# A selective-scan kernel on Trainium2: summing over the states by accumulating fp32 transposes

## The chip, the cores and the metric

The kernel runs on one core of a Trainium2 chip. The metric is the device time of one execution in microseconds (us). A core has five engines that run side by side and wait for each other by semaphores: TensorE (PE; its weight loads are listed apart as PEld), VectorE (DVE), ScalarE (ACT), GpSimd (POOL) and SyncE (SP), which here only issues transfers. TensorE writes to PSUM, an accumulator memory of eight banks of 128 partitions x 512 fp32 values; a matmul holds one operand still in the array (it is loaded first) and streams the other through it.

## The reference, cut to what matters

Eight images of 96 channels and 64 x 64 pixels pass through a Mamba-like layer, an attention without softmax and a quantised feed-forward network. Nearly all the time goes to the selective scan of the first layer: 192 inner channels, 4096 positions, four directions and 16 states for each channel.

```python
def step(h, t):
    u_t, d_t, B_t, C_t = t
    dA = jnp.exp(d_t[..., None] * A)
    h = dA * h + (d_t * u_t)[..., None] * B_t[:, :, None, :]
    y = jnp.einsum('bkdn,bkn->bkd', h, C_t)
    return (h, y)
```

Here n runs over the 16 states. The change concerns the last sum: y is the sum over n of h times C.

## The kernel before, in words

The images go in four pairs. For each pair, `front` does the norms, the input projection and the depthwise convolution, `scan` the selective scan in four directions, `back` the output norm, gate and projection, and `tail` the attention and feed-forward network. The 192 channels of two images fill three tiles of 128 partitions.

`scan` cuts the 4096 positions into 8 chunks of 512. A step is one chunk in one direction, so there are 32 steps for a pair; each step has three tiles T and each tile 16 states n. The innermost piece of work, a unit, is one (step, tile, state): 48 units make a step, 6144 the kernel. A unit has three parts:

- `unit_a`: two bf16 matmuls spread row n of B and of C over the 128 partitions, into the PSUM tiles pb (L322) and pcc (L324). ScalarE computes da, the exponential of delta times A (L326), VectorE multiplies pb by du in place (L329), and ScalarE copies pcc to cc in SBUF (L331).
- `unit_b`: VectorE runs the recurrence over the 512 positions as one scan instruction (L342), GpSimd multiplies the result by cc, which gives hc (L344), and after every fourth state ScalarE saves the last column (L347).
- `unit_c`: TensorE adds hc to the PSUM tile py by a matmul with the identity (L352). After the 16th state VectorE adds py to y (L357 in the first direction, L362 in the others).

The loop at the end of `scan` hands out part a of unit i, part b of unit i - 1 and part c of unit i - 3. Between the units it slips in what the next tile or step needs: `project` makes B and C and the low-rank step input of a new step with two sets of three fp32 matmuls (L268), ScalarE's copies (L272, L277), VectorE's split into bfloat16 parts (L274, L278) and one GpSimd subtraction (L279). `step_size` makes delta and du for one tile with a small fp32 matmul ptd (L285), five ScalarE functions (L290 to L297), one VectorE instruction (L299) and three GpSimd products (L300, L301, L303).

A scheduler of the framework orders each engine's instructions, and every engine then runs its list in that order. In the list of TensorE, pb stands four units ahead of py: after py of unit i comes pb of unit i + 4, often with a pcc beside it. Buffers limit how far the engines drift apart: pb has three PSUM banks, pcc and py two each, and the eighth bank, tag "m", is shared by the projections and ptd; da, cc and hc have three SBUF buffers each.

Of the kernel before, what the change touches and what calls it, by code (L numbers as in the profile page):

```python
# [21 lines left out]
NS = 16  # L22
# [10 lines left out]

# Two images share three 128-partition tiles of the 192 inner channels:
#   tile 0: image 0, channels 0..127      tile 1: image 1, channels 0..127
#   tile 2: channels 128..191 of image 0 (partitions 0..63) and of image 1 (64..127)


@with_exitstack
def vss_attn_ffn(ctx: ExitStack, tc: tile.TileContext, a: dict):  # L40
# [11 lines left out]

    # one table set for all but Silu
    nc.scalar.preload_act_table_set(LOGEXP)
# [29 lines left out]

    # A = -exp(A_log); the sum over the directions of D, as all four read the same u
    amat = load("alog", [128, KD, 2, NS])
# [4 lines left out]

    # FFN weights and biases in the 5-bit exponent, 2-bit mantissa format
    w1q = const.tile([DIM, HID], F8, name="w1q")
# [23 lines left out]

# [1 line left out]
    def front(pair, xi, zs, ybuf):  # L119
        with ExitStack() as st:  # L120
# [52 lines left out]

            # Silu from here on, in a table set of its own
            for b in range(2):
# [51 lines left out]

# [1 line left out]
    def scan(xi, y):  # L229
        with ExitStack() as st:  # L230
# [8 lines left out]
            def view(t, k, c):  # L239
                """Chunk c of an image in the order of direction k (before its flip)."""  # L240
                if k % 2 == 0:
                    return t[:, bass.ts(c, F)].rearrange("p (h w) -> p h w", w=HH)
                return t.rearrange("p (h w) -> p w h", w=HH)[:, bass.ts(c, ROWS), :]
# [16 lines left out]
            def project(s, g):  # L260
                """B (g = 0, with the step's low rank) or C: rows 0..31, 64..95 and 96..127 of S
                get the high, middle and low bfloat16 parts, whose sum is the float32 value."""
                k, c, _ = steps[s]
                if g == 0:
                    S[s] = pr.tile([128, 2, F], BF16, name="S", bufs=2)
                pt = psm.tile([128, F], F32, name="pt", tag="m")
                for T in range(3):
                    nc.tensor.matmul(  # L268
                        pt, xw[k][:, g, T, :], view(xi[T], k, c), start=(T == 0), stop=(T == 2)
                    )  # L270
                Sg = S[s][:, g]
                nc.scalar.activation(Sg, pt, AF.Copy)  # L272
                R = pr.tile([128, F], F32, name="R")
                nc.vector.tensor_tensor(R[64:128], pt[64:128], Sg[64:128], ALU.subtract)  # L274
                if g == 0:
                    dts[s] = pr.tile([128, F], F32, name="dts")
                    nc.scalar.activation(dts[s][32:44], pt[32:44], AF.Copy)  # L277
                nc.vector.tensor_copy(Sg[64:128], R[64:128])  # L278
                nc.gpsimd.tensor_tensor(Sg[96:128], R[96:128], Sg[96:128], ALU.subtract)  # L279

            def step_size(s, T):
                """delta = softplus(dts + bias) = max(v, 0) + log1p(exp(-|v|)), and delta * u."""
                k, c, _ = steps[s]
                pt = psm.tile([128, F], F32, name="ptd", tag="m")
                nc.tensor.matmul(  # L285
                    pt, dtw[k][32:44, T, :], dts[s][32:44], start=True, stop=True
                )
                bias = dtb[:, k, half(T) : half(T) + 1]
                r = pr.tile([128, F], F32, name="r")
                nc.scalar.activation(r, pt, AF.Relu, bias=bias)  # L290
                e = pr.tile([128, F], F32, name="e")
                nc.scalar.activation(e, pt, AF.Abs, bias=bias)  # L292
                nc.scalar.activation(e, e, AF.Exp, scale=-1.0)
                u = pr.tile([128, F], F32, name="u")
                nc.scalar.activation(u, e, AF.Identity, bias=1.0)
                d = pr.tile([128, F], F32, name="delta", bufs=2)
                nc.scalar.activation(d, u, AF.Ln)  # L297
                # what 1 + e lost in rounding
                nc.vector.scalar_tensor_tensor(u, u, -1.0, e, ALU.add, ALU.subtract)  # L299
                nc.gpsimd.tensor_tensor(d, d, u, ALU.subtract)  # L300
                nc.gpsimd.tensor_tensor(d, d, r, ALU.add)  # L301
                q = pr.tile([128, F], F32, name="du", bufs=2)
                nc.gpsimd.tensor_tensor(rows(q), rows(d), view(xi[T], k, c), ALU.mult)  # L303
                delta[s, T], du[s, T] = d, q

            def feed(s, T):
                """What must have run before tile T of step s, in parts."""
                if s >= len(steps):
                    return []
                k, _, first = steps[s]  # L310
                parts = []
                if T == 0:
                    if first:
                        weights(k)
                    parts += [lambda: project(s, 0), lambda: project(s, 1)]
                return parts + [lambda: step_size(s, T)]

            def unit_a(s, T, n):
                """dA = exp(delta A), dB u = delta u B in PSUM, and C spread over the partitions."""
                k = steps[s][0]  # L320
# [28 lines left out]

            def unit_c(s, T, n, py, hc):  # L350
                k, c, _ = steps[s]
                nc.tensor.matmul(py, ident, hc, start=(n == 0), stop=(n == NS - 1))  # L352
                if n < NS - 1:
                    return
                yv = view(y[T], k, c)
                if k == 0:
                    nc.vector.scalar_tensor_tensor(  # L357
                        yv, view(xi[T], k, c), dsum[:, half(T) : half(T) + 1], rows(py),
                        ALU.mult, ALU.add,
                    )  # L360
                else:
                    nc.vector.tensor_tensor(yv, yv, rows(py), ALU.add)  # L362

# [27 lines left out]

# [1 line left out]
    def back(pair, y, zs, t1):  # L393
        with ExitStack() as st:
# [5 lines left out]
            def mix(m, srcs, T, ps):  # L400
                """The matrices of m take the tiles that hold tile T's images to tile T."""
                use = {0: ((0, 0), (1, 2)), 1: ((0, 1), (2, 2)), 2: ((3, 0), (4, 1), (5, 2))}[T]
                for i, (w, t) in enumerate(use):
                    nc.tensor.matmul(
                        ps, m[:, w, :], srcs[t], start=(i == 0), stop=(i == len(use) - 1)
                    )
# [40 lines left out]

# [1 line left out]
    def tail(pair, t1):  # L449
        with ExitStack() as st:  # L450
# [19 lines left out]

            # a row of ones under the tokens carries the biases
            tn = [big.tile([DIM + 1, L], F32, name=f"tn{b}") for b in range(2)]
            for b in range(2):
                nc.gpsimd.memset(tn[b][DIM : DIM + 1], 1.0)

            # (q k') v = q (k' v): transposed, (k' v)' = v' k for all heads at once
            pm = [psm.tile([128, F], F32, name=f"pm{b}", tag=f"pm{b}") for b in range(2)]
            nblk = L // 128
            for c in range(NCH):
                for b in range(2):  # L480
                    norm(t1[b][:, bass.ts(c, F)], tn[b][0:DIM, bass.ts(c, F)])
                for b in range(2):
                    for i in range(2 * c, 2 * c + 2):
# [10 lines left out]
                        for j in range(2):  # L494
# [3 lines left out]
                            )  # L498
            # the heads' blocks, times the scale; then Wq (k' v) Wff as one matrix
            hm = []  # L500
# [45 lines left out]

            # three chunks at a time, each one part behind the one before it
            going = []
# [6 lines left out]
    for pair in range(npair):  # L555
        zs = dram.tile([3, 128, L], F32, name="zs")
        with tc.tile_pool(name="yp", bufs=1) as yp:
            # the zero-padded input of the convolution, and then the scan's sums
            ybuf = [yp.tile([128, (HH + 2) ** 2], F32, name=f"y{T}") for T in range(3)]
            y = [t[:, :L] for t in ybuf]  # L560
            with tc.tile_pool(name="xip", bufs=1) as xp:
                xi = [xp.tile([128, L], F32, name=f"xi{T}") for T in range(3)]
                front(pair, xi, zs, ybuf)
                scan(xi, y)
            with tc.tile_pool(name="t1p", bufs=1) as tp:
                t1 = [tp.tile([DIM, L], F32, name=f"t1_{b}") for b in range(2)]
                back(pair, y, zs, t1)
                tail(pair, t1)
# [3 lines left out]
def _lay_out(i):  # L572
# [4 lines left out]
    def two(v):  # L577
        """[192, ...] -> [128, 2, ...]: channels 0..127, and 128..191 twice."""
        v = np.asarray(v, f)
# [56 lines left out]

    # constants of the shapes
    e = np.arange(DIM)
# [44 lines left out]
```

## Time and profile before

| | before |
|---|---|
| median of 2 runs | 16719.02 us (16713.03 to 16725.01) |
| span of the profiled execution | 16699.4 us |
| busy: PE, DVE, ACT, POOL | 84%, 76%, 59%, 59% |
| mean granted TensorE clock | 0.906 |
| the four scans together | 13317 us |

The profiled execution's span, from its first to its last instruction, is 16699.4 us, some 20 us below the median of the runs; the difference is what lies around the program. The granted clock is the share of TensorE's full clock that its throttle lets through; in the records it is 1.0 or 0.5 at any one time. An fp32 matmul appears in the trace as two records, each with a weight load of its own, and py of one unit is such a pair. Busy time of TensorE is modelled from the starts of the matmuls and reads too high; distances from start to start tell more.

### The profile page before, as it was taken

The numbers are of one execution on the slowest core, as the hardware profiler recorded it, in microseconds if no ns is written. First come the engines' busy times: TensorE is split into PE (matmuls) and PEld (weight loads), VectorE is DVE, ScalarE is ACT, GpSimd is POOL, SyncE is SP. The second block draws the span as 40 slices with busy tenths as digits, with TensorE's granted clock in tenths as the row PEclk, the third lists the DMA queues.
The fourth block names the chain that finished last, engine by engine and source line by source line (L and its number), as shares of the span: only waits on it lengthen the run. The fifth ranks groups of instructions, "written<-read, shape, count | busy, mean of one in ns | idle before, by whom it ended". The sixth has DMA issues, their size and how long they took to land. (4 is left out here: it accounts for less than half of the span.)

```text
span 16699.4 us, 126308 instructions
## 1 busy us (share of the span) xinstructions
PE 14068.0 (84%) x32636; PEld 4820.2 (29%) x32640; DVE 12648.8 (76%) x14809; ACT 9813.3 (59%) x17754; POOL 9871.6 (59%) x7738
## 2 busy tenths in 40 slices
PE   8888888888988888888898888888889888888888
PEld 2222222223222222222332222222233222222223
DVE  0898899883189889988318988998830898899883
ACT  2666666663266666666326666666632666666663
POOL 0677777772067777777106777777710677777771
PEclk9999999997799999999779999999977999999997
DMA  1000000000000000000000000000000000000001
GB/s 31 2 2 1 2 1 1 1 1 29 24 2 2 1 1 1 1 1 0 30 24 2 2 0 2 1 1 1 1 30 26 0 2 0 2 1 1 1 1 31
DMA packets 48735, 106.06 MB, mean 6 GB/s; under 512 B 7075, under 2 KB 7940, under 8 KB 47108
## 3 DMA queue, kind: packets, MB, share of 16 engines
q1 hardware_dynamic: 48004, 97.97, 2.0%
q8 instruction: 256, 4.19, 0.1%
q14 instruction: 475, 3.89, 0.1%
HBM read 60.21 MB, written 37.75 MB: 6 GB/s over the span
## 5 line engine op out<-in xcount | busy, mean ns | idle before, releaser
L344 POOL TENSOR_TENSOR hc<-h,cc 128x512 f32<-128x512 f32 x6144 | 7831.6, 1280 | 3405.2 <-DVE h L342 2561.7
L352 PE MATMUL py<-hc,ident 128*128 128x512 f32 x12288 | 7244.3, 673 | 1992.9 <-POOL hc L344 1968.2
L342 DVE TENSOR_TENSOR_SCAN h<-da,st,pb 128x512 f32<-128x512 f32 x5376 | 6839.4, 1272 | 11.3
L331 ACT ACTIVATE cc<-pcc 128x512 f32<-128x512 f32 x6144 | 3665.9, 597 | 3446.6 <-POOL hc L344 2798.5
L329 DVE TENSOR_TENSOR pb<-pb,du 128x512 f32<-128x512 f32 x6144 | 4184.9, 681 | 1296.2 <-PE pb L322 1268.9
L326 ACT ACTIVATE da<-delta,c_alog 128x512 f32<-128x512 f32 x6144 | 4414.6, 719 | 497.2 <-DVE h L342 461.7
L352 PEld LDWEIGHTS py<-hc,ident 128*128 128x128 f32 x12288 | 2131.0, 202 | 4978.2 <-POOL hc L344 4475.7
L322 PE MATMUL pb<-S,c_sel 128*128 128x512 bf16 x6140 | 2449.9, 399 | 145.1 <-DVE h L342 141.8
L324 PE MATMUL pcc<-S,c_sel 128*128 128x512 bf16 x6144 | 2348.9, 398 | 5.2 <-POOL S L279 2.5
L279 POOL TENSOR_TENSOR S<-R,S 32x512 bf16<-32x512 f32 x256 | 295.7, 1155 | 1838.5 <-DVE S L278 948.1
L324 PEld LDWEIGHTS <-c_sel 128*128 128x128 bf16 x6144 | 628.6, 102 | 2303.6 <-issue 2250.3
L274 DVE TENSOR_TENSOR R<-pt,S 64x512 f32<-64x512 f32 x256 | 177.8, 695 | 1307.3 <-ACT S L272 1300.0
L322 PEld LDWEIGHTS <-c_sel 128*128 128x128 bf16 x6144 | 631.4, 103 | 1777.1 <-issue 1772.9
L268 PE MATMUL pt<-xi,xw 128*128 128x512 f32 x1536 | 1125.5, 825 | 21.1 <-DMA xw<-in_xw_dram 9.9
L342 DVE TENSOR_TENSOR_SCAN h<-da,pb 128x512 f32<-128x512 f32 x768 | 924.6, 1209 | 5.9
L217 PE MATMUL pc<-y,diag 128*128 128x512 f32 x1728 | 748.1, 595 | 0.0
L544 POOL TENSOR_TENSOR ot<-t,y 96x512 f32<-96x512 f32 x64 | 73.5, 1149 | 951.7 <-DVE y L542 936.7
L300 POOL TENSOR_TENSOR delta<-delta,u 128x512 f32<-128x512 f32 x384 | 486.7, 1267 | 155.2 <-DVE u L299 155.2
L303 POOL TENSOR_TENSOR du<-delta,xi 128x512 f32<-128x512 f32 x384 | 535.5, 1394 | 21.3
L301 POOL TENSOR_TENSOR delta<-delta,r 128x512 f32<-128x512 f32 x384 | 486.6, 1267 | 30.1
L222 ACT ACTIVATE xi<-pc,c_convb 128x512 f32<-128x512 f32 x96 | 66.0, 687 | 681.9 <-PE pc L217 681.9
L285 PE MATMUL ptd<-dts,dtw 12*128 12x512 f32 x768 | 439.7, 652 | 25.1 <-ACT e L292 21.2
(115 smaller groups left out, 8068.9 us busy)
## 6 DMA issues: line engine op xcount, KB each, us to landing
z<-zs SPq DMA_DIRECT2D x32, 768.0 KB, 4.9
zs<-zt SPq DMA_DIRECT2D x64, 256.0 KB, 2.0
xt<-in_x_dram SPq DMA_DIRECT2D x8, 1536.0 KB, 9.4
xr<-in_x_dram SPq DMA_DIRECT2D x32, 384.0 KB
out_dram<-ot SPq DMA_DIRECT2D x64, 192.0 KB, 2.1
zs<-zt SPq DMA_DIRECT2D x64, 128.0 KB
xw<-in_xw_dram SPq DMA_DIRECT2D x16, 384.0 KB, 3.1
c_sel<-in_sel_dram SPq DMA_DIRECT2D x1, 1536.0 KB
```

Of the source, the lines that this page charges most:

```text
L217: nc.tensor.matmul(pc, diag[:, half(T), t, :], pad[T][:, r0 + dy : r0 + dy + ROWS, dx : dx + HH], start=(t == 0), stop=(t == 8),)
L268: nc.tensor.matmul(pt, xw[k][:, g, T, :], view(xi[T], k, c), start=(T == 0), stop=(T == 2))
L300: nc.gpsimd.tensor_tensor(d, d, u, ALU.subtract)
L303: nc.gpsimd.tensor_tensor(rows(q), rows(d), view(xi[T], k, c), ALU.mult)
L322: nc.tensor.matmul(pb, sel[:, T, n, :], S[s][:, 0], start=True, stop=True)
L324: nc.tensor.matmul(pc, sel[:, T, n, :], S[s][:, 1], start=True, stop=True)
L326: nc.scalar.activation(da, delta[s, T], AF.Exp, scale=amat[:, k, half(T), n : n + 1])
L329: nc.vector.tensor_tensor(pb, pb, du[s, T], ALU.mult)
L331: nc.scalar.activation(cc, pc, AF.Copy)
L342: nc.vector.tensor_tensor_scan(hs[:, d], da[:, d], pb[:, d], init, ALU.mult, ALU.add)
L344: nc.gpsimd.tensor_tensor(hc, hs, cc, ALU.mult)
L352: nc.tensor.matmul(py, ident, hc, start=(n == 0), stop=(n == NS - 1))
```

## The change

The sum over n is no longer made by multiplying hc with the identity. In the changed kernel hc is the operand that is loaded into the array, in four pieces of 128 columns, and the identity is streamed through, in TensorE's transpose mode; so py collects the transposed pieces, summed over the 16 states. After the 16th state ScalarE copies py to an SBUF tile yt, four more transposes turn it back into a PSUM tile p2, which takes its bank from tag "m", and VectorE adds p2 to y where it added py. Only the first of the 64 transposes of a tile clears the bank.

```diff
             def unit_c(s, T, n, py, hc):
                 k, c, _ = steps[s]
-                nc.tensor.matmul(py, ident, hc, start=(n == 0), stop=(n == NS - 1))
+                for j in range(4):
+                    js = bass.ts(j, 128)
+                    nc.tensor.matmul(
+                        py[:, js], hc[:, js], ident, is_transpose=True, skip_group_check=True,
+                        start=(n == 0 and j == 0), stop=(n == NS - 1),
+                    )
                 if n < NS - 1:
                     return
+                yt = pr.tile([128, F], F32, name="yt")
+                nc.scalar.activation(yt, py, AF.Copy)
+                p2 = psm.tile([128, F], F32, name="p2", tag="m")
+                for j in range(4):
+                    js = bass.ts(j, 128)
+                    nc.tensor.transpose(p2[:, js], yt[:, js], ident)
                 yv = view(y[T], k, c)
                 if k == 0:
                     nc.vector.scalar_tensor_tensor(
-                        yv, view(xi[T], k, c), dsum[:, half(T) : half(T) + 1], rows(py),
+                        yv, view(xi[T], k, c), dsum[:, half(T) : half(T) + 1], rows(p2),
                         ALU.mult, ALU.add,
                     )
                 else:
-                    nc.vector.tensor_tensor(yv, yv, rows(py), ALU.add)
+                    nc.vector.tensor_tensor(yv, yv, rows(p2), ALU.add)
```

The scheduler places the instructions of the changed kernel anew. pb still stands four units ahead of py on TensorE; the back transposes of a tile stand between py of the second and third unit of the tile after it (or beside py of its first unit); the three matmuls of a projection fall between other units than before. GpSimd's list is nearly the same, and SyncE's transfers are the same in number.

## The prediction

> **What bounds the kernel now.** I read the page's busy line first, then the costliest groups, then the waits, then a table by stage, then the timeline of one place where VectorE stands still.
>
> ```profile
> PE 14068.0 (84%) x32636; PEld 4820.2 (29%) x32640; DVE 12648.8 (76%) x14809; ACT 9813.3 (59%) x17754; POOL 9871.6 (59%) x7738
> ...
> L352 PE MATMUL py<-hc,ident 128*128 128x512 f32 x12288 | 7244.3, 673 | 1992.9 <-POOL hc L344 1968.2
> L342 DVE TENSOR_TENSOR_SCAN h<-da,st,pb 128x512 f32<-128x512 f32 x5376 | 6839.4, 1272 | 11.3
> ...
> L329 DVE TENSOR_TENSOR pb<-pb,du 128x512 f32<-128x512 f32 x6144 | 4184.9, 681 | 1296.2 <-PE pb L322 1268.9
> ```
>
> TensorE looks the busiest, but its ends are modelled. VectorE is the engine to follow: its scan never waits (11.3 us), and its product pb*du waits 1268.9 us, all for the matmul that spreads B (L322). The table by stage, first the scan of the first pair of images, then four short stretches and one of the next pair's in_proj:
>
> ```profile
> 453.00:3786.00 3333.00, 2797.67 (x6693) 946.58 (x6694) 2999.36 (x3386) 2197.66 (x4020) 2394.53 (x1884) 0.94 0.00 1
> ...
> 955.10:958.50 3.40, 1.15 (x5) 0.33 (x4) 3.40 (x5) 0.93 (x3) 3.32 (x4) 1.00 0.00 0
> 958.50:961.90 3.40, 2.29 (x5) 0.83 (x6) 2.51 (x3) 2.25 (x6) 3.40 (x3) 0.67 0.00 0
> 961.90:965.30 3.40, 3.40 (x7) 1.11 (x6) 1.88 (x2) 1.88 (x4) 1.30 (x2) 0.50 0.00 0
> 965.30:968.70 3.40, 3.40 (x11) 1.45 (x9) 2.72 (x4) 2.30 (x6) 1.93 (x2) 0.83 0.00 0
> ...
> 4300.00:4400.00 100.00, 100.00 (x103) 20.13 (x102) 0.00 (x0) 35.18 (x52) 0.00 (x0) 0.50 0.17 51
> ```
>
> The column after the five engines is the granted clock. The four scans take 13317 us of the 16699: 6144 units (step, tile, state), 128 steps of 48 units, 104.0 us a step. Undisturbed, scans start 1.77 us apart (957.87 after 956.10), VectorE back to back. So 48 x 1.77 = 85 us, some 9 us of VectorE's other work (L299, L362, L274, L278), and 1268.9/128 = 9.9 us of waiting. Where the waiting comes from, in the timeline:
>
> ```profile
> 958.27 1.27 POOL L303 TENSOR_TENSOR du<-delta,xi 128x512 f32<-128x512 f32 x1
> ...
> 958.37 1.13 PE L352 MATMUL py<-hc,ident 128*128 128x512 f32 x2 [1.91 <-POOL hc L344]
> ...
> 959.74 0.70 DVE L329 TENSOR_TENSOR pb<-pb,du 128x512 f32<-128x512 f32 x1 [0.61 <-PE pb L322]
> ...
> 960.81 2.08 PE L352 MATMUL py<-hc,ident 128*128 128x512 f32 x2 [1.11 <-POOL hc L344]
> ...
> 962.68 0.63 PE L322 MATMUL pb<-S,c_sel 128*128 128x512 bf16 x1
> ...
> 963.35 0.70 DVE L329 TENSOR_TENSOR pb<-pb,du 128x512 f32<-128x512 f32 x1 [1.73 <-PE pb L322]
> ```
>
> GpSimd's three products for the next step size (L300, L301, L303, 3.9 us) hold up hc; TensorE, in order, stands at py; its clock falls to 0.50; the next py then takes 960.81 to 962.68, 1.87 us instead of 0.96 (2006.80 to 2007.76), and pb comes late three times: by 0.61, by 1.73 and, at 965.98, by 0.75: 3.1 us. Three such places a step make up nearly all of the 9.9 us.
>
> **What the skill says.** "TensorE: Matmul & The Clock Gate", Terms, says that the transpose mode is 4 times faster for fp32. The trace has no transpose; the present py is two records, each streaming 512 columns in 0.43 us at full clock, so a quarter of its rate would be one pass of 0.053 us for 128 columns. The same page, section LDWEIGHTS, prices a load by its columns, 107 ns for 128; the trace has 0.107 us between the two loads of one py at full clock, but 0.166 at half. Its Part 4 says that transposes don't count as activity that lifts the clock; no run shows that yet. "PSUM — Partial Sum Buffer", Part "The four PSUM rules", says that an fp32 transpose sets the written bits as a matmul does, so the sum over 16 states should accumulate as meant.
>
> **The change part by part.**
>
> Removed: per unit, one py of 0.96 us at full clock (0.107 of exposed load, 2 x 0.427), 1.87 at half.
>
> Added per unit: four loads of a piece of hc, each with a 128-column matmul. At full clock with loads behind matmuls: 4 x 0.107 + 0.053 = 0.48 us. At half: 0.161 exposed, 3 x 0.166, 0.107: 0.77. Not in the trace are the price of a transpose's pass and whether its load hides. L486, with new weights for each pass, runs 8 passes at 0.16 us each, its loads hidden; that is the lower bound. The upper bound is serial: 4 x (0.107 + 0.053) = 0.64 at full, 4 x (0.166 + 0.107) = 1.09 at half. Two passes as now would double the loads: 8 x 0.107 + 0.107 = 0.96 at full, no gain.
>
> The clock decides. I weighed the trace's matmul records in windows of 3.41 us, streaming time at full clock times the share of rows and columns used. In the scans, all 64 windows at full clock with 0.30 to 0.32 had lost it in the next, and all 24 with 0.42 to 0.44 kept it; at half, none below 0.33 got it back and all above 0.39 did. The last stage line above fits: TensorE 100% busy with 96 rows, clock 0.50. Today a unit in steady state has (0.853 + 0.427)/1.77 = 0.72. After, pb and pcc alone have 0.427/1.77 = 0.24; with transposes counted at one pass, (0.427 + 0.213)/1.77 = 0.36, on the border. I take the scan to be at half clock for most of its length; only the fp32 projections (L268, 0.85 us a matmul at full) lift it for a window.
>
> At half clock a unit then costs TensorE 0.85 for pb and pcc, 0.77 for the transposes and 0.05 for the next load: 1.67 with loads hidden; backlogged serial loads make it 1.93. I take 1.80, nearer to the hidden end, as L486 shows hiding. That is above VectorE's 1.77. Per step: 48 x 1.80 = 86.4; six projection matmuls at 1.71: 10.3; three ptd at 1.87: 5.6; three sets of back transposes at 0.8: 2.4; sum 104.7. Windows lifted by the projections give back some 2. TensorE still stands at py in three bunches, where the queue holds only four pb ahead: 3 x 1.5 = 4.5 not filled. Sum 107.2 against 104.0: +3.2 x 128 = +410 us.
>
> The rest. ScalarE copies yt 384 times at 0.60 (L331's price): 230 us, on an engine 59% busy; it stands behind a cc in the queue, where cc waits for hc anyway. The back transposes wait for yt; behind them on TensorE stand py and pb of the next tile. At two of three tile ends they fall into a bunch, where py waits 3 to 4 us: free. At the third, yt follows cc34 and pb35 stands behind p2: from the scan's end 0.2 + 1.3 + 0.6 + 0.6 + 1.0 + 0.7 = 4.4 us against VectorE's 4.9 until it needs pb35: free by 0.5 us, else up to 1 us a step, 128 us. VectorE's add into y reads p2 instead of py, same size, no cost. p2 shares the single buffer "m" with the projections and ptd, so these now wait for VectorE's add; at unit 33 three projections follow each other behind it, 5 us at half clock, with pb37 behind: 0.5 us of waiting now, up to 2 then. Inside the 1.5 per bunch I count it. Queues of SP and GpSimd keep their work; front, back and tail are not touched.
>
> Span 16699 + 410 = 17109; the runs' median lies 20 above the profiled span: 17130.
>
> **Rivals.**
>
> A, half clock but loads all hidden: TensorE fits into 1.77. The bunches then wait 4 + 2 + 1.1 + 1.5 us a step by the same walk through the queues, 1 more for p2: 9.6 against 9.9, about 16.7 ms, no change. For it: L486. Against it: only 0.10 us of slack a unit in an in-order queue.
>
> B, the clock stays full (transposes count, 0.36 just holds, or a backlog lifts it: 1.28/1.50 = 0.85 at half is above 0.78). Each bunch waits about 1.5 us: 5 a step, 99 us, -640 us: 16.05 ms, faster. If VectorE never waited, 94 us and 15.4 ms: the floor. It decides where the activity is above 0.38. Against it: the skill's sentence and the sum of 0.24.
>
> C, serial loads, or a switch of mode that drains the array: 1.93 a unit: 92.6 + 10.3 + 5.6 + 3.3 + 1 = 113 us a step, +1150: 17.9 ms. Two passes stuck at half clock (8 loads of 0.166): about 2.2 a unit, over 19 ms.
>
> D, the transposes run as two passes at full rate: TensorE as today, clock full; only the back transposes come on top: 16.7 to 17.0.
>
> **How the numbers follow.** The forecast's case 0.35, A 0.2, B 0.22, C 0.15, D 0.08. Slower by over 2% (above 17053, about what a measurement of this kernel tells from no change) takes most of the forecast's case, C and a little of A and D: 0.53. Faster: B, 0.22. Within: 0.25. The range from 16000 to 18300 takes in A, B's main value and C's serial end; the floor and the two-pass end are left out.
>
> **What would show it.** Right: the mean clock of the scan falls from 0.94 to 0.5 to 0.65; transposes come as one load and one matmul each (24576 + 1536 records); VectorE's waiting for pb spreads over all units instead of three bunches. Wrong: scans 1.77 us apart outside the bunches at half clock (A); a clock above 0.8 in the scan (B); 49152 records (C or D); intervals between transposes above 0.27 us.

## The result, and the profile after

The changed kernel takes 16877.08 us (16873.15 to 16881.01, two runs) against 16719.02: a ratio of 1.0093, 95% interval 1.0063 to 1.0122. It is slower, but by less than the 2% from which the prediction counted its chances. Its profiled execution spans 16871.2 us against 16699.4, 172 more. (Each listed run takes only some 2 us longer than its span; the 20 us between the span before and the median of its runs come from one execution to the next, then, and not from what lies around the program.) The four scans hold the loss: from the first to the last scan instruction of each pair, 13320 us before and 13489 after, 169 more.

The busy line and the costliest groups of the page after (columns as before: busy us, mean ns | idle us ahead of the group, releaser):

```profile
PE 12396.1 (73%) x46460; PEld 5923.0 (35%) x46464; DVE 12550.7 (74%) x14809; ACT 10035.9 (59%) x18138; POOL 9908.5 (59%) x7738
...
L355 PE MATMUL py<-ident,hc 128*128 128x128 f32 x24576 | 4557.9, 314 | 3826.1 <-POOL hc L344 3811.3
L342 DVE TENSOR_TENSOR_SCAN h<-da,st,pb 128x512 f32<-128x512 f32 x5376 | 6825.7, 1271 | 10.4
...
L329 DVE TENSOR_TENSOR pb<-pb,du 128x512 f32<-128x512 f32 x6144 | 4179.4, 682 | 1544.4 <-PE pb L322 1518.3
```

The sum itself became cheap: TensorE's busy time falls from 14068.0 to 12396.1 us although it has 42% more records, and py is 24576 records, one pass for each transpose. Yet VectorE's product (L329) waits longer for pb: 1518.3 us, not 1268.9. The table by stage, scan of the first pair:

```profile
453.00:3786.00 3333.00, 2350.09 (x10003) 1206.28 (x10003) 2932.71 (x3340) 2226.10 (x4066) 2374.98 (x1861) 0.88 0.00 1
```

The granted clock in the scan is 0.88, before 0.94: lower, but far from one half. VectorE is busy 2932.71 us of the 3333, before 2999.36: less is done in the same stretch. Where it stands is shown by the timeline of one bunch of GpSimd products (start us, length us, engine, line; in brackets the idle time before and what ended it):

```profile
980.41 1.26 POOL L303 TENSOR_TENSOR du<-delta,xi 128x512 f32<-128x512 f32 x1
...
982.95 0.66 PE L355 MATMUL py<-ident,hc 128*128 128x128 f32 x4 [3.62 <-POOL hc L344]
...
983.44 0.38 PE L324 MATMUL pcc<-S,c_sel 128*128 128x512 bf16 x1
...
983.75 1.99 PE L285 MATMUL ptd<-dts,dtw 12*128 12x512 f32 x2
...
985.67 0.61 PE L322 MATMUL pb<-S,c_sel 128*128 128x512 bf16 x1
...
986.31 0.70 DVE L329 TENSOR_TENSOR pb<-pb,du 128x512 f32<-128x512 f32 x1 [3.18 <-PE pb L322]
...
986.49 1.06 PE L355 MATMUL py<-ident,hc 128*128 128x128 f32 x4
```

GpSimd's bunch keeps TensorE waiting 3.62 us. Then four transposes pass in 0.49 us (982.95 to 983.44), where the identity matmul took 0.96. But the next in TensorE's list is not pb: the new list has pcc and the step size's matmul ptd there, and ptd, at half clock by then, lasts until 985.67. VectorE waits 3.18 us for the pb behind it. At 986.49 four transposes at half clock take 0.86 us to the next start (their last end is modelled).

One more line moved, unasked: the VectorE instruction L299, before and then after:

```profile
L299 DVE SCALAR_TENSOR_TENSOR u<-u,e 128x512 f32<-128x512 f32 x384 | 404.0, 1052 | 20.3 <-ACT delta L297 20.3
```

```profile
L299 DVE SCALAR_TENSOR_TENSOR u<-u,e 128x512 f32<-128x512 f32 x384 | 299.0, 779 | 22.8 <-ACT delta L297 22.8
```

So the books of the scans are: VectorE's idle time between its instructions (gaps of over 40 ns) rises from 1296 to 1561 us (+265), L299 gives back 105, which leaves +160 of the 169.

### The profile page after: what moved, and what is told of

It is laid out like the page before. It is cut to its first block, busy times and chain, and to the rows that moved or that the text cites. A ratio compares the mean times of both kernels' runs of the same rounds, so it can differ in the third digit from the quotient of the medians.

```text
span 16871.2 us, 154492 instructions
## 1 busy us (share of the span) xinstructions
PE 12396.1 (73%) x46460; PEld 5923.0 (35%) x46464; DVE 12550.7 (74%) x14809; ACT 10035.9 (59%) x18138; POOL 9908.5 (59%) x7738
## 5 line engine op out<-in xcount | busy, mean ns | idle before, releaser
L344 POOL TENSOR_TENSOR hc<-h,cc 128x512 f32<-128x512 f32 x6144 | 7867.6, 1287 | 3681.0 <-DVE h L342 2834.4
L355 PE MATMUL py<-ident,hc 128*128 128x128 f32 x24576 | 4557.9, 314 | 3826.1 <-POOL hc L344 3811.3
L342 DVE TENSOR_TENSOR_SCAN h<-da,st,pb 128x512 f32<-128x512 f32 x5376 | 6825.7, 1271 | 10.4
L355 PEld LDWEIGHTS py<-ident,hc 128*128 128x128 f32 x24576 | 3154.2, 158 | 6835.0 <-POOL hc L344 6298.2
L329 DVE TENSOR_TENSOR pb<-pb,du 128x512 f32<-128x512 f32 x6144 | 4179.4, 682 | 1544.4 <-PE pb L322 1518.3
L322 PE MATMUL pb<-S,c_sel 128*128 128x512 bf16 x6140 | 2618.1, 426 | 75.7 <-DVE h L342 71.3
L324 PE MATMUL pcc<-S,c_sel 128*128 128x512 bf16 x6144 | 2608.2, 430 | 22.9 <-ACT cc L331 5.9
L279 POOL TENSOR_TENSOR S<-R,S 32x512 bf16<-32x512 f32 x256 | 295.8, 1156 | 1796.8 <-DVE S L278 1381.0
L322 PEld LDWEIGHTS <-c_sel 128*128 128x128 bf16 x6144 | 656.0, 107 | 913.4 <-issue 607.8
L342 DVE TENSOR_TENSOR_SCAN h<-da,pb 128x512 f32<-128x512 f32 x768 | 926.5, 1209 | 1.1
L324 PEld LDWEIGHTS <-c_sel 128*128 128x128 bf16 x6144 | 666.3, 108 | 247.9 <-issue 169.0
L285 PE MATMUL ptd<-dts,dtw 12*128 12x512 f32 x768 | 585.8, 851 | 26.9 <-ACT e L292 21.2
L217 PEld LDWEIGHTS pc<-y,diag 128*128 128x128 f32 x1728 | 328.6, 190 | 423.6 <-issue 423.6
```

The lines of the kernel that those rows point to most:

```text
L217: nc.tensor.matmul(pc, diag[:, half(T), t, :], pad[T][:, r0 + dy : r0 + dy + ROWS, dx : dx + HH], start=(t == 0), stop=(t == 8),)
L285: nc.tensor.matmul(pt, dtw[k][32:44, T, :], dts[s][32:44], start=True, stop=True)
L322: nc.tensor.matmul(pb, sel[:, T, n, :], S[s][:, 0], start=True, stop=True)
L324: nc.tensor.matmul(pc, sel[:, T, n, :], S[s][:, 1], start=True, stop=True)
L329: nc.vector.tensor_tensor(pb, pb, du[s, T], ALU.mult)
L342: nc.vector.tensor_tensor_scan(hs[:, d], da[:, d], pb[:, d], init, ALU.mult, ALU.add)
```

## The experiments

The theory after the result: the change does two things. Its operations make TensorE's sum shorter, which gains time. It also makes the scheduler lay out new lists, in which more stands ahead of pb where TensorE comes late out of a bunch, which costs more than the gain. The rival: the lists don't matter, and the operations themselves (the lower clock, the way back through yt and p2) cost the 158 us.

To tell these apart, the order of each engine's instructions in `scan` is fixed by edges without semaphores, along a list written into the kernel:

```diff
+            for e, kinds in ORDER.items():
+                ...
+                    if last is not None:
+                        tc.add_manual_dep(i, last.name, ...)
+                    last = i
```

"Old order" is the list of the kernel before for each engine, "new order" that of the kernel after. The recording moves lines by 13: L342 is there what L329 was, L335 the pb matmul, L337 pcc, L298 ptd, L355 the scan, L357 hc, L368 py, L379 p2. TensorE's lists are shown by letters: b for pb, c for pcc, y for the py of one unit, d for ptd, t for one projection matmul. Each ratio is to runs of the kernel before on the same chip, whose medians there lie between 16709 and 16717. No run has only the edges, around an unchanged list, so that they cost nothing by themselves is not shown; the numbers of instructions are the same with them (14809 on VectorE, 17754 on ScalarE, 7738 on GpSimd, before as in e1 and e2).

### The operations and the order, separately

e1 and e3 leave out the way back: no yt, no p2, VectorE adds py, whose blocks are still transposed, to y. e2 has the identity matmuls of before in the new order.

```diff
-                yt = pr.tile([128, F], F32, name="yt")
-                nc.scalar.activation(yt, py, AF.Copy)
-                p2 = psm.tile([128, F], F32, name="p2", tag="m")
-                ...
-                    nc.vector.tensor_tensor(yv, yv, rows(p2), ALU.add)
+                    nc.vector.tensor_tensor(yv, yv, rows(py), ALU.add)
```

> The forward transposes alone (yt and the back transposes are left out, so y receives py in transposed blocks), with every engine's instructions in exactly the order of the kernel before. If the new order of the queues is what costs (ptd and the projections now stand in front of pb where TensorE comes out of a bunch): clearly faster than before, 16.1 to 16.5 ms. If the transposes themselves bring no gain (lower clock, a drain between modes): 16.7 to 16.9 ms. If the back part is what costs: somewhat faster than before, about 16.5 ms.

> The identity matmuls of before, with every engine's instructions in the order of the changed kernel (its yt and back transposes taken out of the order). If the order costs: slower than before by 2% or more, 17.0 to 17.4 ms. If it is the transposes' price or the clock, or the back part: as before, 16.7 ms.

> The forward transposes alone (yt and the back transposes left out), in the order of the changed kernel. If the back part costs nothing: as the changed kernel, 16.88 ms. If the wait for yt and p2 is the loss: 16.5 ms or less.

| | old order | new order | order alone |
|---|---|---|---|
| identity matmuls | 16714.94 (before, on the same chip) | 17360.18, ratio 1.0390 [1.0372, 1.0407] | +645 |
| transposes, no way back | 16266.76, ratio 0.9734 [0.9720, 0.9749] | 16976.27, ratio 1.0160 [1.0145, 1.0176] | +710 |
| transposes alone | -448 | -384 | |

The new order costs 645 to 710 us whatever sums over the states; the transposes gain 384 to 448. The page of e2, then of e1, shows it at the same line:

```profile
L342 DVE TENSOR_TENSOR pb<-pb,du 128x512 f32<-128x512 f32 x6144 | 4200.2, 684 | 2047.5 <-PE pb L335 2010.7
```

```profile
L342 DVE TENSOR_TENSOR pb<-pb,du 128x512 f32<-128x512 f32 x6144 | 4177.5, 680 | 892.6 <-PE pb L335 862.7
```

VectorE's wait for pb is 2010.7 us with the identity in the new order and 862.7 with transposes in the old one, against 1268.9 before. The clock in the scans goes the other way, as the stage lines of e2 and then e1 show:

```profile
453.00:3786.00 3333.00, 2703.30 (x6381) 914.79 (x6382) 2838.15 (x3226) 2117.33 (x3836) 2292.59 (x1797) 0.93 0.00 1
```

```profile
453.00:3786.00 3333.00, 2328.69 (x10014) 1214.27 (x10014) 3026.30 (x3439) 2233.10 (x4084) 2419.77 (x1905) 0.89 0.01 4
```

The slow kernel has the higher mean clock, 0.93 against 0.89, so the mean clock does not decide between these two. With the same sum, though, the new order has the lower clock: 0.93 against 0.94 with the identity, 0.87 (e3) against 0.89 with transposes. And in a bunch the clock is part of the order's cost: ptd takes 1.92 us at half clock in the timeline above, and 1.05 at full clock in the kernel before (2009.85 to 2010.90). How much of the 645 to 710 us this makes was not separated. e3 meets neither of its two expectations; that it lies above the kernel after is taken up below.

### The full change in the old order

e5 has everything of the change, in the old order. Its p2 shares a bank with py instead of the bank of the projections, since the old list has no room for it there:

```diff
-                p2 = psm.tile([128, F], F32, name="p2", tag="m")
+                p2 = psy.tile([128, F], F32, name="p2", tag="y")
```

> The complete change (forward transposes, yt, back transposes), with the instructions in the order of the kernel before. So that this order is possible, p2 takes the second bank of py instead of bank m; the back transposes of a tile stand right in front of the first py of the next tile, yt behind the third cc of the next tile. If only the order was the loss: 16.25 to 16.4 ms, little above the forward transposes alone in the old order (16.27), as the back part lies where TensorE has room. If the back part has a price of its own (wait for yt in front of py and pb): 16.5 ms or more.

16446.9 us, ratio 0.9843 [0.9829, 0.9858]: the change is faster by 1.6% if the order stays. It lies between its two expectations. So the 158 us of the result are -272 for the operations with the way back (-263 against the runs of before on the same chip), and +430 for the new order (16447 to 16877). The +430 takes in the other bank of p2. That rival was not run by itself, but the trace of the kernel after shows little of it: TensorE's matmuls there wait 2.3 us for VectorE's add ahead of a ptd, and not measurably ahead of a projection. The way back costs 180 here (from e1's 16267). VectorE's add waits 298.5 us for p2, which it did not in e1, and its product waits 125 less for pb (862.7 to 737.9), 174 together:

```profile
L342 DVE TENSOR_TENSOR pb<-pb,du 128x512 f32<-128x512 f32 x6144 | 4165.1, 678 | 769.9 <-PE pb L335 737.9
...
L387 DVE TENSOR_TENSOR y<-y,p 128x512 f32<-128x512 f32 x288 | 311.4, 1081 | 298.9 <-PE p L379 298.5
```

In the new order, where VectorE's list has the add later, the add waits 55.4 us, and the kernel after is even 99 us below e3; why the way back is worth a gain there stays open (the clock over the scans is 0.88 in the kernel after and 0.87 in e3).

### What of the new order costs

e4 is the kernel after with ptd set behind the next pb in most places (74 of a pair's 96); e8 also sets pcc behind it; e9 also the projections (125 of the 159 a pair that stood between a py and a pb).

```diff
 TensorE's list, kernel after, then e4, then e8
-  c d b c y
+  c b d c y
-  y c b
+  y b c
```

> The complete changed kernel in its own order, but in nearly all steps each ptd moved behind the pb that followed it in TensorE's queue, and nothing else. VectorE waits 277 us of the changed kernel while ptd runs. If the order costs: 16.5 to 16.65 ms, below before. If it is the transposes' price, the clock or the back part: 16.85 to 16.9 ms.

> The changed kernel with each ptd behind the next pb as in the run with ptd moved (16.69 ms), and in addition pcc moved behind pb wherever it stood between py and pb, since pcc waits there for ScalarE's cc and holds pb up. If the order explains the rest of the way to the old order: 16.4 to 16.6 ms. If not: 16.7 ms.

> The kernel after, with its own order of the queues on the other engines; on TensorE the step size's matmul (L285), the spread of C (L324) and now also the projections (L268), wherever they stood between the transposes of one unit and the next spread of B (L322), stand behind that spread. The run before it moved the first two and took 16640. Theory (what is queued ahead of the spread of B costs its length once TensorE comes late out of a bunch): VectorE's idle time with L268 running was some 240 us of the scans; most of it goes: 16.42 to 16.50 ms, about the kernel with the old order (16447). Rival (the projections are late anyway and something else takes their place, the low-rank copy or the next step size): 16.60 to 16.65 ms.

e4 takes 16687.5 (0.9985 [0.9978, 0.9992]), e8 16639.55 (0.9960 [0.9945, 0.9975]), e9 16675.98 (0.9980 [0.9972, 0.9988]). ptd ahead of pb cost 190 us, pcc about 48; both are less than was expected if the order explains all. The reason given for e8 does not hold either: in the kernel after pcc waits only 5.9 us for cc in all, and what makes up the 48 us was not taken apart. Moving the projections too brought no gain, 36 us the wrong way. Counting units by the scans that VectorE has begun in a step, its wait at unit 20 of the 48 fell by 1.1 us, half of that came back at units 21 to 23, and the wait at unit 37, where the new list has three projections in a row, rose by 0.8: behind one pb the projections are ahead of the next, and come later themselves (VectorE's L287, which splits their result, waits 1428.4 us in e9 and 1292.4 in e8). So e8 and e9 remain some 200 us above e5, and that part had to be looked for elsewhere. The timeline of e8 at the third bunch of a step:

```profile
1160.10 1.26 POOL L316 TENSOR_TENSOR du<-delta,xi 128x512 f32<-128x512 f32 x1
...
1162.63 1.12 PE L368 MATMUL py<-ident,hc 128*128 128x128 f32 x4 [2.38 <-POOL hc L357]
...
1163.54 0.63 PE L335 MATMUL pb<-S,c_sel 128*128 128x512 bf16 x1
...
1164.21 0.70 DVE L342 TENSOR_TENSOR pb<-pb,du 128x512 f32<-128x512 f32 x1 [1.58 <-PE pb L335]
```

Here nothing stands between py and pb any more, and VectorE still waits 1.58 us: by this timeline the three products in one go are long enough by themselves. In the old order GpSimd has an hc between the second and the third. e12 gave e8 GpSimd's old list, e15 only that hc:

```diff
 GpSimd's list, third bunch of a step, e8 and then e15 (0, 1, 3: L300, L301, L303; h: one hc)
-  h 0 1 3 h h
+  h 0 1 h 3 h
```

> The kernel with L285 and L324 behind the spread of B (16640), and GpSimd's instructions in the order of the kernel before; ScalarE, VectorE and TensorE keep the order of that run. In the old order GpSimd has an hc between its second and third product (L301, L303) in the third bunch of a step, and the two differences of the projections (L279) stand at other units. Theory (this holds what is left of the new order's cost, some 190 us, VectorE waiting 1.7 us a step at unit 45 and 0.9 at 37): 16.45 to 16.55 ms. Rival (what is left sits in TensorE's or ScalarE's order, the projections three in a row and the places of the step size's activations): 16.60 to 16.68 ms, no change.

> The kernel with L285 and L324 behind the spread of B (16640), with one change: in the third bunch of a step an hc stands between L301 and L303, as in the old order; L279 stays where it is. VectorE waits 1.8 us a step at units 45 and 46 in that kernel and 1.3 in the change in the old order. Theory: 0.3 to 0.8 us a step, 40 to 100 us less: 16.54 to 16.60 ms; the 208 us more of the last run then came from L279 being earlier. Rival: no change or more, over 16.62 ms, since the hc only shifts the wait to the next units.

e12 is slower, 16847.11 (1.0083 [1.0066, 1.0100]): the old list also has the second L279 of a step, the last piece of a projection, one unit earlier (in 22 of a pair's 32 steps; two units in 6), and a new wait of 1.7 us a step appears at units 39 and 40. It meets neither of its expectations. e15 takes 16593.67 (0.9926 [0.9911, 0.9941]), 46 us less than e8; so the hc gains, and the 253 us between e15 and e12 come with the rest of the old list, which is mainly the other place of L279 (the third bunch also stands two units later in four steps of a pair). One engine's list from one order did not fit the others' lists from another here. The 147 us from e15 to e5 were not taken apart further.

### The bunches taken apart

If the order costs only where TensorE comes late out of a bunch, it should matter little without bunches. e6 and e7 spread GpSimd's three products over several units, in the kernel before (e6) and in e5 (e7):

```diff
 GpSimd's list: at most places, then at the step's end
-  h 0 1 3 h h h h h h
+  h 0 h h h 1 h h h 3
-  h 0 1 h 3 h h
+  h 0 h h 1 h 3
```

> The kernel before in its own order, except that GpSimd's three products for the next step size (L300, L301, L303) no longer follow each other: after most hc three units lie between them (near the end of a step two and one). If the waits of VectorE come from these bunches and the half clock after them: most of its 1296 us of waiting go, 15.5 to 15.9 ms. If TensorE is simply short of throughput: 16.5 ms or more.

> The complete change in the old order as in the kernel with p2 in a bank of py, with GpSimd's three products spread as well. If the bunches are what makes the price of py matter: within 1% of the identity kernel with spread products, 15.5 to 15.8 ms, the transposes then gaining little. If TensorE's throughput matters of itself: 0.4 ms or more below that kernel.

e6 takes 16378.23 (0.9802 [0.9787, 0.9817]), e7 16465.15 (0.9856 [0.9839, 0.9872]). Neither reaches what was expected of it, and e7 is 87 us above e6 and 18 above e5. The wait for pb falls to 548 us in e6 and to 325 in e7, and a new wait for ScalarE's da takes its place once a step (336 us in e6, 338 in e7; e7 also keeps a wait of 334 us of VectorE's add for p2). The timeline of e6:

```profile
1578.78 0.69 ACT L303 ACTIVATE r<-ptd,c_dtb 128x512 f32<-128x512 f32 x1 [7.39 <-POOL delta L314]
...
1580.11 1.28 DVE L355 TENSOR_TENSOR_SCAN h<-da,st,pb 128x512 f32<-128x512 f32 x1 [3.42 <-ACT da L339]
```

r has one buffer; ScalarE can't write the next one before GpSimd has read it in the second product, and stands still for 7.39 us with da queued behind. So the second product should not be late there. e10 (identity) and e11 (full change) set it one unit behind the first in the first eight units of a step, and at its end; e11 also moves VectorE's add two scans later, away from its wait for p2.

```diff
 GpSimd's list in the first units of a step
-  h 0 h h h 1 h h h 3
+  h 0 h 1 h h h 3 h h
 GpSimd's list at the step's end
-  h 0 h h 1 h 3
+  h 0 h 1 h 3 h
 VectorE's list of e11 (m: product, s: scan, y: add)
-  s y m s m s m
+  s m s m s y m
```

> The kernel before (identity matmuls, its own order of the queues), with GpSimd's three products for the next step size (L300, L301, L303) set apart, behind hc of one, three and three further units as in the first such run, but with the second of them only one unit behind the first in the first eight units of a step, since there ScalarE stood still for the one buffer of r. Theory: the first such run had 558 us of waiting for pb and 336 for ScalarE left; the 336 go: 15.95 to 16.1 ms, and the clock in the scans stays over 0.95. Rival (VectorE's own work is the bound by then, or the short distance brings the bunch back): 16.3 to 16.4 ms as before.

> The full change in the old order of the queues, p2 in a second bank of py's, GpSimd's three products set apart in the same way as in the identity kernel beside it, and VectorE's add into y two scans later, so that it no longer waits for the transposes back. Without these two it took 16447, with the first distances 16465. Theory: the wait of the add (some 330 us of VectorE's idle time) and the wait for ScalarE go: 15.8 to 16.0 ms, and against the identity kernel beside it the transposes are then worth little, within 150 us either way, since no bunch is left that the shorter sum could drain faster. Rival (the clock, lower with the transposes, decides once VectorE does not wait for bunches): 16.2 to 16.4 ms, slower than the identity kernel.

e10 takes 15841.29 (0.9479 [0.9463, 0.9495]), e11 15708.83 (0.9398 [0.9384, 0.9412]), on the same chip. e11 beats both kernels, by 6.0% the one before. The stage line of e10, then that of e11 with its wait for pb:

```profile
453.00:3786.00 3333.00, 2851.89 (x7234) 984.50 (x7235) 3054.53 (x3464) 2266.98 (x4158) 2439.30 (x1914) 0.98 0.01 4
```

```profile
453.00:3786.00 3333.00, 2449.47 (x10751) 1311.27 (x10788) 3044.39 (x3486) 2324.93 (x4279) 2445.04 (x1915) 0.90 0.01 4
```

```profile
L342 DVE TENSOR_TENSOR pb<-pb,du 128x512 f32<-128x512 f32 x6144 | 4179.6, 681 | 390.3 <-PE pb L335 331.6
```

With the bunches apart the two ways of summing differ by 132 us (15841 to 15709), not by the 270 of before; they differ in the place of the add as well, so this is not the transposes' share alone. The clock is 0.90 with transposes against 0.98, and again the kernel with the lower clock is the faster one.

e13 and e14 then put the same spread into the new order: e13 is the kernel after with GpSimd's products apart, e14 is e8 with them apart.

> The kernel after with its own order on TensorE, ScalarE and VectorE (the step size's matmul and the projections ahead of the spread of B); only GpSimd's L300, L301 and L303 stand apart, at the distances of the two fastest runs. Theory (the order costs only where TensorE comes late out of a bunch): with no bunch left its cost goes, 15.75 to 15.95 ms, within 250 us of the same change in the old order (15709). Rival (what stands ahead of the spread of B costs wherever it stands): 16.1 to 16.3 ms, the old order's 15709 and the 430 of before.

> As the run beside it, and the step size's matmul (L285) and the spread of C (L324) behind the spread of B, which brought 232 us while the bunches stood. Theory: without bunches the move brings under 60 us against the run beside it. Rival: it brings 150 to 250 us as before.

e13 takes 15917.26 (0.9521 [0.9506, 0.9535]), e14 15808.96 (0.9460 [0.9444, 0.9475]).

```profile
L342 DVE TENSOR_TENSOR pb<-pb,du 128x512 f32<-128x512 f32 x6144 | 4168.5, 680 | 615.5 <-PE pb L335 570.9
```

In e13, whose line this is, VectorE's wait for pb is 570.9 us against 1518.3 in the kernel after, with TensorE's list untouched. Between the new order and the old lie 208 us now (15917 to 15709), before 430: by this comparison half of the order's cost existed only behind the bunches. It is not a clean one, since e11 also has VectorE's add later than e5. The other half is for the most part at two places of a step: unit 41, where ptd stands ahead of pb (VectorE waits 1.3 us there in e13, and 0.5 at units 41 and 42 in e14; 128 steps times 0.8 make 102 of the 108 us between them), and unit 37 with three projections in a row (1.0 us in e14, 0.2 in e11; 128 times 0.8 again, against 100 between these two). The match is rough: all of VectorE's idle time in the scans rises by 146 us from e11 to e14, and L299 gives back 51. So neither expectation of e14 was met in full: what stands ahead of pb costs less without bunches, but not nothing.

## Why the prediction was wrong

Slower was right, but by luck. The size, +410 us against +158, was wrong, and so was the path to it: the clock term failed (point 2), and with it the unit of 1.80 us at half clock (point 3); and the term that decides, the new order of TensorE's list, was left out (point 5).

1. **The price of the transposes**: 0.48 us for a unit at full clock; measured 0.49 (982.95 to 983.44), of which all but the first transpose take 0.11 from start to start (0.109 is the median of the trace, 0.213 at half clock). The sum is right, its parts are not. I took the Trainium skill ("TensorE: Matmul & The Clock Gate", Terms, four times faster for fp32) as 0.053 us of streaming behind a load of 0.107. The measured interval, with the loads hidden, is one pass of 128 columns at the rate of either pass of py before (0.43 us for 512 columns at full clock, 0.85 at half; a quarter is 0.107 and 0.213). So a transpose needs one pass where the matmul needs two, at the same rate: twice as fast, not four times.
2. **The clock term failed.** I took the scan at half clock for most of its length, mean 0.5 to 0.65. It is 0.882 over the scans: 3184 us at half clock, before 1672. Part 4 of that page says that the full clock does not engage for transposes (its measurement there is of bf16); here fp32 transposes count. Weighing the records of the kernel after in windows of 3.41 us as before, a transpose counted with 0.107 us puts the threshold between full and half clock in the next window at 0.37, the value that the kernel before gives too, and misplaces 30 of the scans' 3949 windows; counted with nothing, the best threshold misplaces 473, with 0.053 us 185. A unit at full clock then weighs (0.427 + 4 x 0.107)/1.77 = 0.48, safely above 0.37, where I had 0.24 to 0.36. The measured clock is the sign I had named for rival B.
3. **The unit of 1.80 us** therefore hardly occurs, and with it the 104.7 us of TensorE per step. Even at half clock four transposes take 0.85 us (986.49 to 987.35) and the two spreads 0.82 (985.67 to 986.49), 1.7 in all and not 1.80: of 666 distances from scan to scan that lie wholly at half clock, 305 are at most 1.79 us and only 4 between 1.79 and 1.85. VectorE stays the bound outside the bunches (980.09 to 981.86 from scan to scan, 1.77 us), and its waiting stays in a few places.
4. **The waits in the bunches** were sized at 1.5 us each, 4.5 a step. In the new order VectorE waits 11.9 us a step for pb (1518.3/128). In the old order it is 6.7 in e1 (862.7/128): rival B's mechanism, 1.7 above the 5 that I put there. So B's 16.05 ms is nearly met by e1 (16.27) and not by the kernel after.
5. **The new order of TensorE's list, for which the sum has no term, is what decides**: +430 us. The one place that the prediction names, the projections behind p2 at unit 33, is put at nothing ("Inside the 1.5 per bunch I count it"), and no sum of it has ptd between py and pb (three ptd a step, 5.6 us, stand only in the total of TensorE's time). A walk along the new list out of the bunch shown above would have had it: py 0.49, pcc 0.31, ptd 1.92 at half clock, pb 0.64. These 3.36 us are what VectorE's 3.18 us of waiting at 986.31 consist of.
6. **The way back** was put between free and 128 us; with VectorE's add at no cost; in the old order it is 180, with 298.5 of waiting at just that add; in the new order the kernel with it is 99 us faster than e3 without it.

So the sign came out right by two errors that offset each other: a loss to half clock that did not come, and a loss to the order that was left out. The operations by themselves gained (-272 us in e5), where the prediction had them lose.

## What to carry to other kernels

Where a scheduler writes the lists, a change of one operation is also a change of the order, and the order alone moved this kernel by 3.9% (e2). Take the new list of the late engine, start at the instruction that ends a long wait, and add up everything ahead of the first result that the bounding engine needs. And take the bunch apart before making the work behind it cheaper: spreading three products of another engine brought 5.2% with the old sum, and the new sum 0.8% on top, with one add moved as well.

## What the runs showed of the hardware

- fp32 transposes that accumulate in PSUM take 0.109 us per 128 columns at full clock and 0.213 at half, from start to start, and in this kernel count for the granted clock with 0.107 us (point 2 above).
- A higher granted clock goes with the slower kernel in three pairs: 0.93 in e2 (17360 us) and 0.89 in e1 (16267), 0.94 before and 0.90 in e5, 0.98 in e10 and 0.90 in e11. In each of these the sums differ; with the same sum it is the other way round, if by little (0.94 before and 0.93 in e2, 0.89 in e1 and 0.87 in e3). The mean clock did not rank these kernels.
- The VectorE instruction L299 comes in two durations: in the kernel before 218 of 384 at 0.73 us and 166 at 1.48 in the mean, after 332 at 0.67 and 52 at 1.49. The identity kernel in the new order (e2) has the same split as the kernel after, and the transposes in the old order (e1) nearly that of the kernel before (216 and 168). It depends on the order, then, and not on the sum; with the way back in the old order (e5) it is 273 and 111. What makes it slow stays open: GpSimd's product L344 runs beside all the slow ones before and after, but beside nearly all the fast ones too.
